# A fused attention and feed-forward kernel on one Trainium2 core: in the first block, big loads wait for TensorE's products, and the block's steps are written in a new order

## The chip, the cores and the metric

The kernel runs on one core of one Trainium2 chip. The metric is the device time of one execution in microseconds (us). TensorE (PE) multiplies matrices, VectorE (DVE), ScalarE (ACT) and GpSimd (POOL) work element by element; SyncE (SP), ACT and POOL also issue DMAs.

## What is computed

`x` is 32 x 64 x 512, float32. Two stages follow one another, each on a layer norm of its input and each added to its input:

```python
x = x + xattn(layernorm(x), ctx, ctx, Wq, bq, Wk, bk, Wv, bv, Wo, bo)
x = x + ffn(layernorm(x), gate, up, down)
# xattn, for every sample: q = Wq x + bq, k = Wk c + bk, v = Wv c + bv   (64 x 64 weights)
#   8 heads over the 512 columns: p = softmax(q_h k_h^T / 8), 64 x 64;  out = Wo (p v_h) + bo
# ffn: each weight is (int32 - int32 zero) * scale, zeros and scales per group of 128 rows
#   out = (silu(h gate) * (h up)) down,   gate, up: 512 x 1792, down: 1792 x 512
```

## The kernel before

Two samples make a pair (128 partitions: 2 x 64 rows), there are 16 pairs, and four pairs make a block of 512 rows (PB = 4), so four blocks. For each block the kernel runs attention, then the feed-forward stage; the attention of block t + 1 is threaded into the feed-forward of block t, which takes 14 slices of 128 columns (gate_up, L588, and down, L629). The first block has no feed-forward to hide in, and its attention is done alone: that is the part that the change touches.

**The first block.** Its steps are methods of class Attention (L322), one object for each of the pairs 0 to 3: stats, scale, apply (layer norm on DVE, the power on POOL, DVE); k, q, v (projections on PE) with k_out, q_out (DVE) and v_out (ACT); scores (PE), highest and less (DVE), exp (ACT), sums (DVE), divide (POOL); turn (PE: weights of the softmax, transposed, times Wo) and turn_out (ACT); weigh (PE), residual (DVE, and a DMA of x1 to DRAM from SP); stats2, scale2, apply2 (second layer norm); flip (PE transposes), high (ACT) and low (DVE), which leave the transposed input of the feed-forward stage in two parts hTh and hTl, so that the float32 product is done as two. PE products take four PSUM tiles of two banks in turn (pool ps0).

**The written order.** The string START (L734) lists these steps with the pair's number, and the loop at L774 issues them one by one under a manual schedule: each engine gets its instructions in this order, and each engine works its own queue in order. Names without a number are common steps: projections, biases and scales prepare constants; zeros (zeros_to_dram, L147) casts the zero points on POOL, writes them to DRAM from SP and, in the kernel before, also issues the broadcast load of the first 512 columns' zeros to all partitions (load_zeros, L272: three DMAs from SP, 512, 512 and 256 KB) and the rows of x of the next two pairs (load_rows, L123: one DMA of 512 KB from SP); weights (load_weights, L265) issues three DMAs of 1 MB each from POOL, one behind the other: the integers of gate, up and down for the first 512 of the 1792 columns; integers is one step of weight_steps (L286): POOL subtracts the zeros from a 128 x 512 piece of gate or up (four such steps stand near the end of START); quotients (L232) prepares scale ratios on DVE.

**After the first block** the order within each engine comes from the framework's planner, which goes by the order of the program text and by its own estimates of times. A few calls pin instructions behind others (issue_after); `newest` keeps, for each engine, the last instruction of the first block's steps or of the main loop, behind which POOL's later loads and subtractions are put. Down's pieces are subtracted on DVE (L301), gate's and up's on POOL (L295), each block of 512 columns after its zeros have been reloaded into the one buffer z.

Of the kernel before, what the change touches and what calls it, by code (L numbers as in the profile page):

```python
# [1 line left out]

# [24 lines left out]
def kernel(  # L27
# [41 lines left out]
    nc = tc.nc  # L69
    B, D, L = x.shape  # L70
    I = gate_w.shape[1]
    P = 128
# [5 lines left out]
    PB = 4  # L78
    NBLK = NPAIR // PB
    TB = PB * P  # L80
    SET = 2
# [32 lines left out]
    with ExitStack() as fast:  # L114
        const = fast.enter_context(tc.tile_pool(name="const", bufs=1))
        rows = fast.enter_context(tc.tile_pool(name="rows", bufs=1))
        att = fast.enter_context(tc.tile_pool(name="att", bufs=1))
        blk = fast.enter_context(tc.tile_pool(name="blk", bufs=2))
        zeros = fast.enter_context(tc.tile_pool(name="zeros", bufs=1))
        xs, hTh, hTl = {}, {}, {}  # L120
        newest = {}

        def load_rows(j: int, pairs: list = [range(SET)]):  # L123

            xs[j] = rows.tile([P, SET, L], F32, tag="x", name=f"x_{j}", bufs=3)
            for some in pairs:
                load_pairs(xs[j], x_rows, j, some)

        def load_pairs(dst: bass.AP, src: bass.AP, j: int, some: range):
            a, b = some.start, some.stop  # L130
            return nc.sync.dma_start(dst[:, a:b, :], src[:, j * SET + a : j * SET + b, :]).ins
# [5 lines left out]
        def places(pool):  # L137
            return {n: pool.tile([P, SET, L], F32, tag=n, name=f"{n}_set") for n in PARTS}
# [27 lines left out]
        wide = [(c, min(CW, I - c)) for c in range(0, I, CW)]  # L166
# [3 lines left out]
        def projection_loads():  # L170
            w_nat = early.tile([D, 5, D], F32, tag="w_nat", name="w_nat")
            b_nat = early.tile([1, 6, D], F32, tag="b_nat", name="b_nat")
            for i, w in enumerate((Wk, Wv, Wq, Wo)):
                nc.scalar.dma_start(w_nat[:, i, :], w)
            for i, b in ((1, bk), (0, bq), (2, bv), (4, bo)):
                nc.gpsimd.dma_start(b_nat[:, i, :], b.unsqueeze(0))
            nc.gpsimd.tensor_copy(w_nat[:, 4, :], w_nat[:, 0, :])
            for i in (2, 4):
                nc.scalar.copy(b_nat[:, i + 1, :], b_nat[:, i, :])
            return w_nat, b_nat  # L180
# [37 lines left out]
        def scale_loads():  # L218
            s_nat = early.tile([NS, 3, P], F32, tag="s_nat", name="s_nat")
            for m, s in enumerate((gate_s, up_s, down_s)):  # L220
                nc.sync.dma_start(s_nat[:, m, :], s.rearrange("g (c p) -> (g c) p", p=P))
            return s_nat
# [33 lines left out]
        ng = const.tile([P, KT, I], F32R, tag="ng", name="ng")  # L256
        nu = const.tile([P, KT, I], F32R, tag="nu", name="nu")
        nd = const.tile([P, FC, L], F32R, tag="nd", name="nd")
        n_sum = []

        gate_rows = gate_w.rearrange("(g p) i -> p g i", p=P)
        up_rows = up_w.rearrange("(g p) i -> p g i", p=P)
        down_rows = down_w.rearrange("(f p) l -> p f l", p=P)

        def load_weights(at: int, n: int):  # L265

            c, fs = slice(at, at + n), slice(at // P, (at + n) // P)
            nc.gpsimd.dma_start(ng[:, :, c], gate_rows[:, :, c])
            nc.gpsimd.dma_start(nu[:, :, c], up_rows[:, :, c])
            newest["POOL"] = nc.gpsimd.dma_start(nd[:, fs, :], down_rows[:, fs, :]).ins  # L270

        def load_zeros(at: int, n: int):  # L272
            z16 = zeros.tile([P, 2, KT, CW], BF16, tag="z16", name=f"z16_{at}")
            z8 = zeros.tile([P, KT, CW], U8, tag="z8", name=f"z8_{at}")
            for m in range(2):
                nc.sync.dma_start(
                    z16[:, m, :, :n], z_rows[m, :, at : at + n].partition_broadcast(P)
                )
            nf = n // P
            zd = z8_dram[at // P * L : (at // P + nf) * L]  # L280
            nc.sync.dma_start(
                z8[:, :nf, :].rearrange("p f l -> p (f l)"), zd.partition_broadcast(P)
            )
            return z16, z8

        def weight_steps(zs):  # L286

            for i, (at, n) in enumerate(wide):
                if i:
                    zs = load_zeros(at, n)  # L290
                z16, z8 = zs
                for g in range(KT):
                    for m, dst in enumerate((ng, nu)):
                        piece = dst[:, g, at : at + n]
                        nc.gpsimd.tensor_tensor(  # L295
                            piece, piece.bitcast(F32), z16[:, m, g, :n], ALU.subtract
                        )
                        yield
                for i in range(n // P):
                    piece = nd[:, at // P + i, :]  # L300
                    nc.vector.tensor_tensor(piece, piece.bitcast(F32), z8[:, i, :], ALU.subtract)  # L301
                    yield
# [424 lines left out]
        def chain(*gens):  # L727
# [4 lines left out]


        START = """  # L734
            0.stats 0.scale 0.apply 1.stats projections 1.scale biases 1.apply
            projections_out 2.stats 0.k biases_out 2.scale 3.stats 0.q 1.k 0.q_out
            3.scale 1.q 0.k_out zeros 2.apply 0.scores 1.q_out 2.k 0.highest 0.less
            2.k_out 0.exp 1.k_out 0.sums 2.q 3.apply 3.k 0.divide 2.q_out 3.q
            3.k_out weights 2.scores 3.q_out 0.turn 2.highest 3.scores 0.turn_out
            2.less 1.scores 3.highest 2.exp 3.v 3.less 1.highest 0.v 3.exp 1.less  # L740
            3.v_out scales 2.sums 1.v 0.v_out 1.exp 3.sums 2.v 2.divide 1.v_out
            0.weigh 1.sums 3.divide scales_out 2.v_out 0.residual 0.stats2 2.turn
            1.divide 3.turn 2.turn_out 2.weigh 3.turn_out quotients 0.scale2 1.turn
            2.residual 2.stats2 3.weigh 1.turn_out 1.weigh 1.residual 1.stats2
            2.scale2 0.apply2 1.scale2 2.apply2 0.flip 3.residual 3.stats2 2.flip
            0.high 2.high 1.apply2 3.scale2 integers integers integers integers
            0.low 1.flip 3.apply2 2.low 1.high 3.flip 1.low 3.high 3.low
        """
        place = places(att)
        with (  # L750
            tc.tile_pool(name="early", bufs=1) as early,
            tc.tile_pool(name="att0", bufs=1) as att0,
            tc.tile_pool(name="ps0", bufs=4, space=bass.MemoryType.PSUM) as ps0,
            tc.manual_schedule(),
        ):
            w_nat, b_nat = projection_loads()
            at_first = [place, places(att0)]
            for j in range(PB // SET):
                load_rows(j, [])
            for p in range(PB):  # L760
                j, i = divmod(p, SET)
                load_pairs(xs[j], x_rows, j, range(i, i + 1))
                load_pairs(at_first[j]["c"], c_rows, j, range(i, i + 1))
            for m, z in enumerate((gate_z, up_z, down_z)):
                nc.sync.dma_start(z_nat[:, m, :], z.rearrange("g (c p) -> (g c) p", p=P))
            s_nat = scale_loads()
            make_block(0)

            def first_banks(name: str):
                return ps0.tile([P, 2, CW], F32, tag="s", name=name)  # L770

            pairs = [Attention(p, 1, at_first[p // SET], first_banks) for p in range(PB)]
            halves = {}
            for step in START.split():  # L774
                if step[0].isdigit():
                    getattr(pairs[int(step[0])], step[2:])()
                elif step == "weights":
                    load_weights(*wide[0])
                elif step == "zeros":
                    zeros_to_dram()  # L780
                    weights = weight_steps(load_zeros(*wide[0]))
                    load_rows(PB // SET)
                elif step == "integers":
                    next(weights)
                elif step == "quotients":
                    quotients()
                elif step.endswith("_out"):
                    next(halves[step[:-4]], None)
                else:
                    halves[step] = {  # L790
                        "projections": lambda: projections(w_nat),
                        "biases": lambda: biases(b_nat),
                        "scales": lambda: scales(s_nat),
                    }[step]()
                    next(halves[step])
# [70 lines left out]
    with tc.If(nc.values_load(flag, min_val=0, max_val=1) != 0), ExitStack() as slow:  # L866
# [20 lines left out]
        for at, n in wide:  # L887
            c = slice(at, at + n)
# [86 lines left out]
```

## Time and profile before

| what | value |
|---|---|
| median of 3 runs | 458.27 us (457.67 to 458.99) |
| profiled execution, own time | 457.47 us |
| its span, first to last instruction | 454.7 us |
| mean granted TensorE clock | 0.97 of full |
| busy: PE, DVE, ACT, POOL | 414.0, 331.5, 309.1, 280.0 us |
| last hTl of the first block, on DVE | starts at 44.11, takes 0.69 us |
| first product of the feed-forward stage, on PE | starts at 44.90 us |
| three weight loads of the first block issued on POOL | at 18.18, 19.03, 19.78 us |
| zeros' broadcast, rows of x issued on SP | at 12.82 to 13.87, at 14.37 us |

The profile is of one execution. Busy time says how long an engine had an instruction in work; a wait is put down to what released it, and "issue" is idle time in which an engine waited for nothing that the profile shows. In the page's slices each digit is a fortieth of the span (11.4 us), in tenths. The page's chain follows the work that ended last back from the end. Where the busy times of stretches are shown, the columns are: the stretch, its length, then busy us (and count of instructions) of PE, of PE's weight loads, of DVE, ACT and POOL, then the granted clock, the mean share of 16 DMA engines and GB/s. DMA queues are q1 (issued from SP), q0 (issued from POOL) and q8 (kind "instruction").

### The profile page before, as it was taken

Reading aid. Unit: us, or ns where it says so; the run is one execution under the profiler, and the core shown is the slowest. Engines: PE = TensorE matmul, PEld = TensorE weight load, DVE = VectorE, ACT = ScalarE, POOL = GpSimd, SP = SyncE. Lnnn points to the kernel's source line nnn. Section 1 sums busy time; section 2 is a strip of 40 time slices with the busy share of each in tenths; the row PEclk is TensorE's granted clock in tenths of the full one; section 3 lists DMA queues with packets and bytes.
Section 4 is the critical chain, followed back from the end, with each engine's and each line's share of the span. In section 5 each row is a group of like instructions: output and inputs, shape, how many; then the busy total and the mean of one; then the engine's idle time right before and its main releaser. Section 6 shows DMA issues by size and latency. Waiting matters only on the chain.

```text
span 454.7 us, 10323 instructions
## 1 busy us (share of the span) xinstructions
PE 414.0 (91%) x4175; PEld 316.3 (70%) x4175; DVE 331.5 (73%) x510; ACT 309.1 (68%) x473; POOL 280.0 (62%) x293
## 2 busy tenths in 40 slices
PE   4755998998999999999999899999999999999991
PEld 4743564766677776777778577786778888887871
DVE  4878653797979983696869775586869655668673
ACT  2142589665787669686788569786688778777760
POOL 5335739658474487676787686764566887783311
PEclk9885899999999999999999999999999999999997
DMA  6793779436102020141000012130001012100004
GB/s 207 234 306 137 217 227 257 130 105 183 54 22 77 1 94 1 46 140 50 1 16 32 2 48 94 48 94 1 1 1 48 1 47 86 54 1 0 1 2 146
DMA packets 20928, 36.55 MB, mean 80 GB/s; under 512 B 1848, under 2 KB 7432, under 8 KB 20872
## 3 DMA queue, kind: packets, MB, share of 16 engines
q1 hardware_dynamic: 14056, 24.20, 16.0%
q0 software_dynamic: 6208, 11.01, 8.6%
q8 instruction: 35, 0.57, 0.5%
q10 hardware_dynamic: 608, 0.59, 0.4%
q14 instruction: 21, 0.17, 0.1%
HBM read 27.37 MB, written 8.42 MB: 79 GB/s over the span
## 4 chain that ended last, share of the span: by engine, by line
PE 43%; POOL 25%; issue 14%; DVE 10%; DMA 3%; ACT 3%; ACTq 0%; POOLq 0%; SPq 0%; DVEq 0%
PE pu L597 10%; PE pg L597 10%; POOL hl L624 7%; PE pd L642 6%; PE pd L645 5%; POOL squares L318 4%; POOL squares L316 4%; POOL hh L623 3%; DVE xn_set L112 3%; DVE y L653 2%; DMA z<-z_dram 2%; POOL q_e_set L481 2%; POOL nu L295 2%; POOL ng L295 1%; DVE k_eT_set L404 1%
## 5 line engine op out<-in xcount | busy, mean ns | idle before, releaser
L653 DVE SCALAR_TENSOR_TENSOR y<-pd,s_all,y 128x512 f32<-128x512 f32 x204 | 150.1, 743 | 47.0 <-PE pd L645 44.2
L607 ACT ACTIVATE pg<-pg,s_q 128x512 f32<-128x512 f32 x168 | 111.5, 665 | 74.2 <-PE pg L597 72.9
L607 ACT ACTIVATE pu<-pu,s_q 128x512 f32<-128x512 f32 x168 | 110.8, 660 | 4.1 <-PE pu L597 4.1
L642 PE MATMUL pd<-hh,nd 128*128 128x512 f32 x224 | 93.9, 419 | 1.6 <-DVE y L653 1.1
L597 PE MATMUL pg<-hTh,ng 128*128 128x512 f32 x224 | 91.2, 407 | 4.5 <-POOL ng L295 1.4
L623 POOL CAST hh<-h 128x512 fp32r<-128x512 f32 x55 | 35.1, 637 | 92.3 <-DVE h L613 90.7
L597 PE MATMUL pu<-hTh,nu 128*128 128x512 f32 x224 | 90.3, 403 | 0.8 <-POOL nu L295 0.5
L597 PE MATMUL pg<-hTl,ng 128*128 128x512 f32 x224 | 89.3, 399 | 0.0
L597 PE MATMUL pu<-hTl,nu 128*128 128x512 f32 x224 | 88.9, 397 | 0.0
L645 PE MATMUL pd<-hl,nd 128*128 128x512 f32 x224 | 88.7, 397 | 0.1
L624 POOL TENSOR_TENSOR hl<-h,hh 128x512 fp32r<-128x512 f32 x55 | 72.0, 1309 | 4.4
L613 DVE SCALAR_TENSOR_TENSOR h<-pu,s_all,g 128x512 f32<-128x512 f32 x56 | 41.8, 747 | 34.3 <-ACT g L610 27.8
L318 POOL TENSOR_TENSOR squares<-squares 128x512 f32<-128x512 f32 (+1 forms) x46 | 55.1, 1197 | 1.7
L597 PEld LDWEIGHTS pg<-hTh,ng 128*128 128x128 f32 x224 | 42.2, 189 | 18.3 <-ACT pg L607 3.9
L642 PEld LDWEIGHTS pd<-hh,nd 128*128 128x128 f32 x224 | 42.0, 188 | 18.0 <-DVE y L653 5.0
L597 PEld LDWEIGHTS pu<-hTh,nu 128*128 128x128 f32 x224 | 42.2, 188 | 13.9 <-ACT pu L607 2.8
L597 PEld LDWEIGHTS pu<-hTl,nu 128*128 128x128 f32 x224 | 42.2, 188 | 9.9 <-issue 0.4
L597 PEld LDWEIGHTS pg<-hTl,ng 128*128 128x128 f32 x224 | 42.4, 189 | 9.0
L610 ACT ACTIVATE g<-pg,s_all 128x512 f32<-128x512 f32 x56 | 38.8, 693 | 13.9 <-PE pg L597 12.1
L645 PEld LDWEIGHTS pd<-hl,nd 128*128 128x128 f32 x224 | 42.1, 188 | 7.9 <-POOL hl L624 0.5
L295 POOL TENSOR_TENSOR ng<-ng,z 128x512 fp32r<-128x512 f32 (+1 forms) x16 | 16.6, 1040 | 8.0 <-DMA z<-z_dram 8.0
L295 POOL TENSOR_TENSOR nu<-nu,z 128x512 fp32r<-128x512 f32 (+1 forms) x16 | 17.1, 1069 | 0.0
(290 smaller groups left out, 484.0 us busy)
## 6 DMA issues: line engine op xcount, KB each, us to landing
z<-z_dram SPq DMA_DIRECT2D x6, 512.0 KB
x<-in_x_dram SPq DMA_DIRECT2D x6, 512.0 KB
ng<-in_L_ffn_gate_w_dram POOLq DMA_DIRECT2D x3, 1024.0 KB, 5.9
nu<-in_L_ffn_up_w_dram POOLq DMA_DIRECT2D x3, 1024.0 KB, 7.7
nd<-in_L_ffn_down_w_dram POOLq DMA_DIRECT2D x3, 1024.0 KB, 10.6
c_set<-in_ctx_dram SPq DMA_DIRECT2D x6, 512.0 KB
x_dram<-x SPq DMA_DIRECT2D x6, 512.0 KB
r<-x_dram SPq DMA_DIRECT2D x6, 512.0 KB
```

The source lines that it names most:

```text
L295: nc.gpsimd.tensor_tensor(piece, piece.bitcast(F32), z16[:, m, g, :n], ALU.subtract)
L316: nc.gpsimd.tensor_tensor(square[:, :n], piece, piece, ALU.mult)
L318: nc.gpsimd.tensor_tensor(total[:, :n], total[:, :n], square[:, :n], ALU.add)
L597: nc.tensor.matmul(acc, w[:, g, ts(f, P)], half[:, g, :], start=(g == 0 and half is hi), stop=(g == KT - 1 and half is lo), skip_group_che ...
L607: nc.scalar.activation(acc, acc, AF.Copy, scale=by)
L610: nc.scalar.activation(g_sb, acc, AF.Silu, scale=by)
L613: ins = nc.vector.scalar_tensor_tensor(h_sb, acc, by, g_sb, ALU.mult, ALU.mult)
L623: nc.gpsimd.tensor_copy(hh, h_sb)
L624: ins = nc.gpsimd.tensor_tensor(hl, h_sb, hh.bitcast(F32), ALU.subtract)
L642: nc.tensor.matmul(pd, w, h_hi[t, f], start=(t, f) != LAST, stop=False, skip_group_check=True)
L645: nc.tensor.matmul(pd, w, h_lo[t, f], start=False, stop=True, skip_group_check=True)
L653: ins = nc.vector.scalar_tensor_tensor(y, pd, by, y, ALU.mult, ALU.add)
```

## The change

The load of the three weights is cut into single steps, gate, up and down; so is what zeros issued: broadcast (the three zeros' DMAs) and rows. Four of them, broadcast, up, rows and down, stand in a context behind_products: the first instruction that they issue gets a true dependency (a semaphore wait) on the last PE instruction traced before it. So in the new order the broadcast waits for 1.scores, up for 3.k, rows for 0.turn and down for 3.turn. Gate has no such wait. On its queue the whole load stands behind its first DMA. START is written anew: pairs 0 and 1 come ahead of pairs 2 and 3 in most steps (before, pair 1's scores and turn came after those of pairs 2 and 3), gate stands where zeros stood and zeros follows it, down is issued late in the block, and the four integers stand ahead of 2.apply2, 3.apply2 and quotients. No operation on data is added or removed.

```diff
+        def load_wide(w: bass.AP, src: bass.AP, at: int, n: int):
+            newest["POOL"] = nc.gpsimd.dma_start(w[:, :, at : at + n], src[:, :, at : at + n]).ins
+
+        def load_down(at: int, n: int):
+            fs = slice(at // P, (at + n) // P)
+            newest["POOL"] = nc.gpsimd.dma_start(nd[:, fs, :], down_rows[:, fs, :]).ins
+
         def load_weights(at: int, n: int):
-            c, fs = slice(at, at + n), slice(at // P, (at + n) // P)
-            nc.gpsimd.dma_start(ng[:, :, c], gate_rows[:, :, c])
-            nc.gpsimd.dma_start(nu[:, :, c], up_rows[:, :, c])
-            newest["POOL"] = nc.gpsimd.dma_start(nd[:, fs, :], down_rows[:, fs, :]).ins
+            load_wide(ng, gate_rows, at, n)
+            load_wide(nu, up_rows, at, n)
+            load_down(at, n)
...
         START = """
-            0.stats 0.scale 0.apply 1.stats projections 1.scale biases 1.apply
-            projections_out 2.stats 0.k biases_out 2.scale 3.stats 0.q 1.k 0.q_out
-            3.scale 1.q 0.k_out zeros 2.apply 0.scores 1.q_out 2.k 0.highest 0.less
-            2.k_out 0.exp 1.k_out 0.sums 2.q 3.apply 3.k 0.divide 2.q_out 3.q
-            3.k_out weights 2.scores 3.q_out 0.turn 2.highest 3.scores 0.turn_out
-            2.less 1.scores 3.highest 2.exp 3.v 3.less 1.highest 0.v 3.exp 1.less
-            3.v_out scales 2.sums 1.v 0.v_out 1.exp 3.sums 2.v 2.divide 1.v_out
-            0.weigh 1.sums 3.divide scales_out 2.v_out 0.residual 0.stats2 2.turn
-            1.divide 3.turn 2.turn_out 2.weigh 3.turn_out quotients 0.scale2 1.turn
-            2.residual 2.stats2 3.weigh 1.turn_out 1.weigh 1.residual 1.stats2
-            2.scale2 0.apply2 1.scale2 2.apply2 0.flip 3.residual 3.stats2 2.flip
-            0.high 2.high 1.apply2 3.scale2 integers integers integers integers
-            0.low 1.flip 3.apply2 2.low 1.high 3.flip 1.low 3.high 3.low
+            0.stats 0.scale 0.apply 1.stats projections 1.scale biases
+            projections_out 1.apply 2.stats 0.k biases_out 2.scale 3.stats 0.q 1.q
+            0.k_out 3.scale 0.q_out 1.k gate zeros 1.q_out 0.scores 1.k_out 2.k
+            3.apply 1.scores broadcast 0.highest 2.apply 2.k_out 0.less 0.v
+            1.highest 0.exp 2.q 1.less 0.v_out 3.q 0.sums 1.exp 2.v 2.q_out 0.divide
+            3.k up 2.v_out 1.sums 2.scores 3.q_out 1.divide 3.k_out 1.v 2.highest
+            3.scores 1.v_out 2.less 1.turn 3.highest 2.exp 0.turn rows 3.less
+            1.turn_out 2.sums 3.exp 1.weigh 0.turn_out 3.sums 2.divide 3.v
+            1.residual 1.stats2 3.divide 0.weigh 3.v_out 2.turn 0.residual 0.stats2
+            1.scale2 3.turn down 2.turn_out 2.weigh 3.turn_out 1.apply2 0.scale2
+            scales 2.residual 2.stats2 3.weigh scales_out 1.flip 3.residual 3.stats2
+            2.scale2 1.high 0.apply2 3.scale2 integers integers integers integers
+            2.apply2 0.flip 1.low 2.flip 3.apply2 0.high quotients 3.flip 2.high
+            0.low 3.high 2.low 3.low
         """
...
+            @contextmanager
+            def behind_products():
+                traced = nc.cur_bb.bb.instructions
+                last = next(i for i in reversed(traced) if i.engine == mybir.EngineType.PE)
+                n = len(traced)
+                yield
+                first = traced[n]
+                tc.add_manual_dep(
+                    first,
+                    last.name,
+                    mybir.DependencyInfo(
+                        mybir.DependencyClass.Sync, mybir.DependencyReason.DATA
+                    ),
+                    reason="behind products",
+                )
...
-                elif step == "weights":
-                    load_weights(*wide[0])
+                elif step == "gate":
+                    load_wide(ng, gate_rows, *wide[0])
                 elif step == "zeros":
                     zeros_to_dram()
-                    weights = weight_steps(load_zeros(*wide[0]))
-                    load_rows(PB // SET)
+                elif step == "broadcast":
+                    with behind_products():
+                        weights = weight_steps(load_zeros(*wide[0]))
+                elif step == "up":
+                    with behind_products():
+                        load_wide(nu, up_rows, *wide[0])
+                elif step == "rows":
+                    with behind_products():
+                        load_rows(PB // SET)
+                elif step == "down":
+                    with behind_products():
+                        load_down(*wide[0])
```

More of the change, by code (lines that the diff above doesn't have):

```diff
@@ L1 @@
-from contextlib import ExitStack
+from contextlib import ExitStack, contextmanager
 import concourse.bass as bass
```

## The prediction

> **What bounds the kernel now.** I read the page's forty slices first, then the chain of work that ended last over the first 46 us, then who waited for whom on VectorE (DVE) there, then busy time by stretch, then the DMA queues of short stretches. Overall TensorE (PE) is busy for 91% of the span, but the change touches only the first 45 us, and there the slices show something else:
>
> ```profile
> PE   4755998998999999999999899999999999999991
> DVE  4878653797979983696869775586869655668673
> PEclk9885899999999999999999999999999999999997
> ```
>
> Slices are 11.4 us wide. In the second PE has 7 tenths and DVE 8; in the third and fourth PE falls to 5, and its granted clock falls with it. The chain says what happens inside:
>
> ```profile
> 28.15 0.47 PE po L506 x32
> 28.62 0.28 PE pe L490 x10
> 28.90 3.48 issue
> 32.38 0.81 PE pe L490 x13
> ```
>
> PE stops after 10 of the 32 products of 1.turn, waits for no semaphore, and goes on 3.48 us later. DVE runs dry behind it (columns: total, times, longest, over 0 to 44.85 us):
>
> ```profile
> DVE st L368 <- DMA x<-in_x_dram: 3.6, 1, 3.6
> DVE x L518 <- PE po L506: 3.4, 1, 3.4
> DVE xn_set L112 <- POOL rs L374: 1.4, 2, 0.8
> DVE mx L455 <- PE pss L444: 1.4, 2, 1.1
> DVE hTl L543 <- ACT hTh L539: 0.6, 1, 0.6
> DVE q_e_set L404 <- PE pq L393: 0.4, 1, 0.4
> ```
>
> These six are all of DVE's idle time in the block: 10.8 us. Everything else is work, so **DVE's queue sets the block's end** (last hTl at 44.11 + 0.69 = 44.80 us; the first gate product starts at 44.90), plus what it waits for.
>
> Why does PE stop? Cutting the stretch where PE has gaps with no releaser (19.99, 26.05, 32.38) gives the matmuls between them:
>
> ```profile
> 0.00:19.95 19.95, 11.42 (x346) 10.51 (x346) 13.76 (x30) 3.04 (x6) 8.96 (x23) 0.95 0.65 207
> 19.95:26.03 6.08, 4.62 (x127) 3.53 (x127) 4.82 (x10) 4.02 (x8) 1.24 (x2) 0.87 1.19 358
> 26.03:32.30 6.27, 2.54 (x126) 2.27 (x127) 5.40 (x15) 1.93 (x4) 3.35 (x5) 0.96 1.09 341
> ```
>
> First two pairs: PE and its weight loads. The gaps stand 127+127 and 126+127 instructions apart: [...]so they are borders of instruction blocks, reached after matmuls 346, 473 and 599. The queue of kind "instruction" (q8) carries such blocks: between 24 and 30 us it has no packet, in 30 to 32 us it has one, while the third big load (down) drains:
>
> ```profile
> q1 hardware_dynamic: 298, 0.56, 74.5%
> q8 instruction: 1, 0.02, 3.0%
> q0 software_dynamic: 11, 0.01, 2.3%
> ```
>
> Before that, q0 alone (three 1 MB weight loads issued back to back at 18.18, 19.03 and 19.78) took 132 and 134% of the engines in 24:26 and 26:28. So the fetch of the block after 599, due when PE passed 473 at 26.05, came after the weights, and too late.
>
> [...] The 3.48 us stop is followed by a clock of 0.50 from 32 to 48 us. [...] Here an apply takes 0.54 us, and 1.29 us at 40.99, beside POOL's integers.
>
> **The change part by part.** I call T0 the end of the last hTl, 44.80 now, and count how it moves.
>
> *The waits on loads.* Counting matmuls in the new order (10 up front; 32 for each k, q, scores, turn, weigh; 8 for a v): 3.k ends at 346, 0.turn covers 451 to 482, 3.turn 587 to 618, 1.scores 203 to 234. If the borders stay at 346, 473 and 599, and one stride earlier at 219, each of the four waiting loads (zeros broadcast behind 1.scores, up behind 3.k, rows behind 0.turn, down behind 3.turn) is issued just after PE has entered a new block, so the fetch is asked for ahead of the load. The block after 599 is then due about 4.3 us after 473: DVE's 3.highest 0.69, 3.less 0.69, 2.sums and 3.sums 0.86 each, then about 1.0 for 3.divide (POOL, 3.04 for three) and part of the turn; now it is 2.8 us. In front of that fetch lie up's rest, rows and context, 0.5 MB each, not 3 MB. I take the stop as gone: **-3.44** on DVE. If part of it stays, cover is under rival B.
>
> *What queues behind the waiting instructions.* On POOL, up holds 1.divide; 3.k follows 2.v with no late input, and 0.divide occupies POOL meanwhile: 0, plus the 0.75 us of the issue itself, which 3.scores covers (1.turn comes after it). Down holds 0.scale2, which nobody needs before 0.apply2, four DVE steps later: 0. Gate's issue (0.85) moves ahead of the casts of the zeros (0.39 and 0.29) and so of their way through DRAM; integers need them some 20 us later: 0. On SP the broadcast (three DMAs) and rows (one) hold the next context load and the writes of x1; the first reader of these is the next block: 0. Without these covers each would cost its own length, 0.7 to 0.9 us.
>
> *The written order.* Pair 1 is now finished early, and between a PE step and its reader on DVE there are one to three other DVE steps. Waits that may go: 0.63 (last hTl; now two lows and quotients stand before) and 1.4 + 0.4 (highest, q_out). The first I count whole, the other two half, since new short waits can appear: **-0.63 - 0.9**; bounds -0.6 and -2.4. The 1.4 of the first applies stays: that part of the order is the same.
>
> *Contention it adds.* integers now stand before 2.apply2, 3.apply2 and quotients; now only one apply runs beside them. One more apply at 1.29 - 0.54 = **+0.75**; quotients (0.23 + 0.68 + 0.24) may double: 0 to 1.15, [...]**+0.3**.
>
> *Clock.* Between the last weigh and T0 PE has only flips in both orders, so the entry is at half clock either way. Now it lasts 4.0 us past T0 (the 2 us from 48 on have a mean clock of 0.79, so full speed returns at about 48.8); [...]the chain there runs through DVE, POOL and DMA, not PE. **+0.2**[...].
>
> Sum: -3.44 - 0.63 - 0.9 + 0.75 + 0.3 + 0.2 = **-3.7 us**. After T0 nothing in the chain is tied to the clock of the start: rs_4to, the next weight issues, integers, the reload of zeros (8.19 us) all hang on T0, so the shift reaches the end. The profiled execution took 457.47 us (span 454.7, 2.8 around it) and would take 453.8; it is 0.8 below the median of 458.27, for which the same step gives **454.5 us**.
>
> **Rivals.** A, the above: 452.0 to 456.2 (the waits all gone, no quotient cost, -5.5, and a little from what is planned after; or only the stop and the 0.63 gone, with half of the unknown costs: -3.44 - 0.63 + 0.75 + 0.55 + 0.7 = -2.1, 456.2). Chance 0.70.
>
> B, the fetch is still late, somewhere in 3.turn, by the whole 3.5 us. DVE then still has 1.stats2's rest, 0.residual 0.87, 0.stats2 1.1 and 1.apply2 0.54, about 2.5 us, before it needs 2.weigh; PE needs 1.0 for the rest of 3.turn and 2.weigh. Cover 1.5, exposed 2.0: 454.5 + 2.0 = 456.5, range 455.5 to 457.3. For it: context and rows are still on the queues then. Against: the borders found above. Chance 0.14.
>
> C, the change doesn't do what it is meant to, or the gain is spent right after T0: the zeros' reload (8.19 us beside 3 MB of weights) ends where it did. Then 458.3, within 457.2 to 459.5. Against: the reload starts on POOL's last nu, which follows T0. Chance 0.10.
>
> D, slower: down is issued last, some 10 us later than now (19.78, against about 28.5, taken from 3.turn's end, 28.15 now). Its reader is DVE's nd subtraction (45.99 now, 1.1 after the first gate product; then about 42.3), and behind it on DVE stands rs_4to, on which POOL's next loads wait. Now down's load of this block lands 11.3 us after issue, behind gate and up; alone it should need less. 28.5 + 0.75 + 11.3 = 40.6, still in time. Each us past 42.3 costs one; it is slower than before from a landing at about 46: at 48, 460.2. Chance 0.06.
>
> **How the numbers follow.** The forecast is A's. Range 452.0 to 457.2: A and B to their ends; C and D, 0.16, are left out. About 0.3% (1.4 us) is what a measurement of this kernel can tell from no change. Faster: A and six sevenths of B, 0.82; same: the rest of B and C, 0.12; slower: D, 0.06.
>
> **What would show it.** Right: no issue gap over 1 us on PE before T0; q8 packets soon after matmuls 346 and 473; DVE's idle time under 7 us, the po wait gone; two applies near 1.3 us; the first gate product near 41 us. Wrong: T0 moves by 4 and the end does not (C); a PE gap inside 2.turn or 3.turn (B); DVE idle at nd for a DMA (D).

## The result, and the profile after

| kernel | median, us (runs, lowest to highest) | ratio to before, 95% interval |
|---|---|---|
| before, same chip | 459.12 (20, 457.62 to 462.02) | |
| after | 457.19 (20, 454.44 to 458.89) | 0.995, 0.9931 to 0.9969 |

The change is worth some 2 us, where 3.7 were forecast. The profiled execution of after took 457.63 us (span 455.3), beside 457.47 (span 454.7) in the one of before that is shown: these two executions do not show the gain at all. The first gate product of the feed-forward stage (a matmul into pg) starts at 43.85, not at 44.90 and not "near 41". The ninth, which opens the second slice of 128 columns, starts at 56.66, against 56.52, and up to the last gate product the distance between the two executions stays at 0.1 us. The spans are 0.6 apart, but they are a poor measure here: the own time less the span is 2.73 us in the mean of the 130 runs of before whose span is on record, and 2.29 in the 44 of after. Own times and starts of products are compared below.

The page's slices of after, the rows PE, DVE and PEclk:

```profile
PE   4854998998999999999999899999999999999991
DVE  5959553797979983696869775586869655668672
PEclk9988799999999999999999999999999999999996
```

The third slice (from 22.8 us) still has PE at 5 tenths, and now DVE is at 5 tenths with it. The chain of waits shows that PE still stops, in another place:

```profile
22.10 0.57 PE pe L497 x23
22.67 5.15 issue
27.82 0.50 PE pe L497 x9
28.32 0.90 PE po L513 x32
29.24 0.89 DVE x L525 x2
```

PE stops after 23 of the 32 products of 0.turn. 0.turn covers matmuls 451 to 482, so this is after 473: the border before the one that stopped it in before. At 599 PE does not stop any more, as was predicted. Who waited for whom on DVE, up to 45 us (total, times, longest):

```profile
DVE x L525 <- PE po L513: 4.3, 1, 4.3
DVE st L375 <- DMA x<-in_x_dram: 3.8, 2, 3.6
DVE xn_set L112 <- POOL rs L381: 1.4, 2, 0.8
DVE k_eT_set L411 <- PE pk L400: 0.2, 1, 0.2
```

The short waits for highest, q_out and the last hTl are gone; the long one has grown from 3.4 to 4.3. The busy times by stretch, cut at border 346, at the stop, at the first and the ninth gate product (columns as under "Time and profile before"):

```profile
0.00:18.70 18.70, 11.15 (x346) 9.78 (x346) 12.99 (x29) 4.92 (x9) 7.35 (x21) 1.00 0.62 186
18.70:22.67 3.97, 3.18 (x127) 2.38 (x128) 3.87 (x8) 1.38 (x4) 2.40 (x3) 1.00 0.91 293
27.82:43.85 16.03, 9.21 (x229) 7.66 (x228) 14.13 (x32) 4.99 (x9) 8.09 (x9) 0.80 0.77 234
43.85:56.66 12.81, 11.71 (x160) 7.27 (x161) 7.45 (x15) 6.21 (x9) 8.28 (x9) 0.73 0.79 220
```

Again 346 and then 127 matmuls, so the borders are where the prediction had them. That a block is fetched one block ahead was read by the prediction from before, and this trace agrees: the next two packets of the queue of kind "instruction" (q8) come at 28.9 and 32.4, 1.1 and 1.0 us after PE has passed 473 (27.82) and 599 (31.40). By this the block after 473 is asked for when PE passes 346, at 18.7. The queues' rows of four stretches, 17 to 18.7, 18.7 to 23, 23 to 25.3 and 25.3 to 27.9 us:

```profile
q1 hardware_dynamic: 18, 0.02, 3.1%
...
q1 hardware_dynamic: 1131, 1.22, 93.4%
...
q0 software_dynamic: 315, 0.65, 88.5%
q1 hardware_dynamic: 51, 0.07, 22.0%
...
q1 hardware_dynamic: 243, 0.48, 53.4%
q0 software_dynamic: 210, 0.40, 47.3%
q8 instruction: 1, 0.02, 2.3%
```

Just ahead of the border the engines are idle. Then the zeros' broadcast (1.22 MB on q1) fills them, then up (q0), and the q8 packet comes 6.6 us after the border, at 25.3 (it ends at 26.25; PE goes on at 27.82). Why these two loads lie there is seen in the issues on SP and POOL (start, length, engine and line, what):

```profile
11.08 0.81 POOL L267 DMA_DIRECT2D ng<-in_L_ffn_gate_w_dram  x1
...
12.33 0.33 SPq L150 DMA_DIRECT2D z_dram<-z  x1
12.76 0.34 SPq L151 DMA_DIRECT2D z_dram<-z  x1
17.24 0.95 SPq L283 DMA_DIRECT2D z<-z_dram  x2
18.29 0.45 SPq L288 DMA_DIRECT2D z<-z_dram  x1
...
19.23 0.82 POOL L267 DMA_DIRECT2D nu<-in_L_ffn_up_w_dram  x1
```

The products of 1.scores, for which the broadcast waits by the change, were through at 14.60. It is issued at 17.24, because it also reads what the zeros wrote to DRAM, and that small write stood behind gate's 1 MB. SP's own waits name it (total, times, longest):

```profile
SPq L283 <- DMA z_dram<-z: 4.1, 1, 4.1
```

And 3.k ends exactly at matmul 346, so the wait of up holds it only to the end of the old block (18.42). POOL was still at a divide, and issued up 0.5 us after PE had passed the border.

### The profile page after: what moved, and what is told of

It is laid out like the page before. It is cut to its first block, busy times and chain, and to the rows that moved or that the text cites. A ratio compares the mean times of both kernels' runs of the same rounds, so it can differ in the third digit from the quotient of the medians.

```text
span 455.3 us, 10322 instructions
## 1 busy us (share of the span) xinstructions
PE 413.0 (91%) x4175; PEld 315.3 (69%) x4175; DVE 330.5 (73%) x510; ACT 309.3 (68%) x473; POOL 280.4 (62%) x293
## 4 chain that ended last, share of the span: by engine, by line
PE 45%; POOL 23%; issue 15%; DVE 10%; ACT 4%; DMA 1%; ACTq 0%; POOLq 0%; DVEq 0%
PE pg L604 11%; PE pu L604 11%; PE pd L649 6%; POOL hl L631 6%; PE pd L652 5%; POOL squares L325 4%; POOL squares L323 4%; POOL hh L630 3%; DVE xn_set L112 2%; DVE y L660 2%; POOL nu L302 2%; POOL q_e_set L488 1%; POOL ng L302 1%; DVE k_eT_set L411 1%; DMA w_nat<-in_L_xattn_Wo_dram 1%
```

## The experiments

In the expectations, theory F is the mechanism of the prediction: the fetch of a block of instructions waits for data that are queued, and PE stops when the block is not there. The other letters are rivals.

**Both kernels profiled again.** Nothing is edited; the question is what varies. The columns: own time of the profiled execution, PE's stops of over 1 us at a border (from the start of the last matmul to that of the next, and after which matmul), start of the first and of the ninth gate product.

| execution | own time | stops | first | ninth |
|---|---|---|---|---|
| before, shown | 457.47 | 3.70 (599) | 44.90 | 56.52 |
| before_again | 458.40 | 3.05 (599) | 43.92 | 57.31 |
| before_third | 457.54 | 2.78 (599) | 42.95 | 56.29 |
| before_fourth | 458.20 | 4.38 (346), 1.37 (473), 1.44 (599) | 45.40 | 57.08 |
| before_fifth | 459.55 | 3.56 (346), 1.98 (599) | 45.61 | 59.00 |
| before_sixth | 457.50 | 3.89 (599) | 44.42 | 55.90 |
| after, shown | 457.63 | 5.36 (473) | 43.85 | 56.66 |
| after_again | 458.05 | 5.90 (473) | 44.65 | 57.35 |
| after_third | 458.41 | 5.09 (473) | 44.37 | 57.10 |
| after_fourth | 455.81 | 5.09 (473) | 43.45 | 54.87 |

> The kernel before once more, for its profile alone: its timed runs go from 456.1 to 462.4 us, and the profile shown is from the fast end (457.47). Theory F: the place of the stop depends on which transfers a block's fetch meets, so another execution shows a stop of another length, 3 to 6 us, after matmul 473 or 599. Theory C [...]: the same stop of 3.5 us after 599, first gate product at 44.9, and a half clock that lasts 4 to 8 us past it.

> The same, once more, with the same expectations: F, a stop of 3 to 6 us in another place or of another length; C, the same stop and only another clock.

> The kernel before, for a profile of one of its longer executions (its runs go up to 462 us, the three profiles so far took 457.5 to 458.4). Theory F: if it takes over 459.5, a stop of 5 us or more, or two stops, between matmuls 346 and 599. Theory C: the stop is 3 us and the clock after it is low for longer.

> The same once more: F, over 459.5 us only with a stop of 5 us or more or two stops; C, with the stop of 3 us and a longer low clock.

> The kernel before once more. Theory F: stops of 3 to 7 us in all, after 346 or 599, first gate product 43 to 46. If its long executions (460 to 462 us) are those with stops at more than one border, one that takes 460 us or more shows over 6 us of stops and a first gate product after 46.

> The changed kernel once more, for how far one profile of it stands for others. Theory F (the fetch of the instruction block after matmul 473 waits behind the zeros' broadcast and the up load, which are issued at 17.2 to 20.1 us, over the border at matmul 346): the same order of transfers, so a PE stop of 4 to 6 us again after matmul 473 and a first gate product at 43 to 45 us. Theory R (the stop is an accident of one execution): another place or no stop. Time 0.992 to 0.998 of the kernel before under both.

> The changed kernel once more, a look at its spread. Theory F: one stop of 5 to 6 us after matmul 473, the first gate product at 43.5 to 45. Rival V (the place of the stop varies as it does in the kernel before, and the medians' 2.3 us come from executions without it): no stop over 3 us, first gate product below 42.

> As after_third: by theory F a stop of 5 to 6 us after matmul 473 and the first gate product at 43.5 to 45; by rival V no such stop and below 42.

In before the place of the stop is a matter of the execution: four times at 599, twice at 346. The chain of before_fourth, where it fell in 0.turn's first half:

```profile
18.55 0.23 PE pe L490 x16
18.78 4.16 issue
22.94 0.71 PE pe L490 x16
```

In after it is at 473 in all four profiles, and 5.1 to 5.9 us long; rival V of after_third (executions without the stop) found no support. Timed again in 22 runs, after had a median of 457.51 us and a ratio of 0.9951 (0.9931 to 0.997). before_sixth did not catch a long execution: before took 460 us or more in 55 of its 150 timed runs, after in 0 of 44, but none of the six traces of before is of such a run. The longest of them, before_fifth with 459.55, has stops over 1.9 us at two borders, which is what theory F had asked of an execution over 459.5.

One thing narrows down where executions differ: in all 20 traces of this document, of every kernel, the own time less the start of the ninth gate product is 400.3 to 401.6 us, and the last gate product starts 380.4 to 380.8 us after the ninth. What made these executions long or short lies ahead of the ninth product.

**Gate and zeros exchanged (zeros_first).** The small write goes ahead of gate's 1 MB.

```diff
-            0.k_out 3.scale 0.q_out 1.k gate zeros 1.q_out 0.scores 1.k_out 2.k
+            0.k_out 3.scale 0.q_out 1.k zeros gate 1.q_out 0.scores 1.k_out 2.k
```

> The changed kernel with zeros ahead of gate, so that the small write of the zeros to DRAM is not behind gate's 1 MB. Theory F: the broadcast goes out at about 14.7 us, right behind 1.scores, drains by about 20, and the fetch asked for at matmul 346 (18.3 us) comes before 22.5: the stop after 473 shrinks from 5.15 us to under 1.5 us, and the first gate product moves from 43.85 to about 41; time 0.988 to 0.993 of before. Rival P (PE's blocks can't come faster than one in so many us, whatever else is on the queues): the stop stays at 4 to 5 us. Rival M (the broadcast now meets gate, and the fetch at matmul 219 is late instead): a stop of 2 us or more after 346, and a gate product at 42 to 44.

Measured: 457.06 us (12 runs), ratio 0.9935 (0.9905 to 0.9965). The broadcast is issued at 14.83, 2.4 us earlier, but now gate is ahead of its data, which drain from 16.7 to 21; up follows. The packet comes at 24.33, and PE's stop after 473 is 4.27 us, of which DVE waits 3.2. This edit takes away a fifth of the stop: border 346 is still under load. Theory F had forecast less than 1.5 us; the number is the one of rival P, which only later runs (mended, weights_late) rule out.

**Up behind rows (up_later).** Only the step up is moved, from 3.k to behind 0.turn and rows.

```diff
-            3.scores 1.v_out 2.less 1.turn 3.highest 2.exp 0.turn rows 3.less
+            3.scores 1.v_out 2.less 1.turn 3.highest 2.exp 0.turn rows up 3.less
```

> The changed kernel with up issued behind 0.turn (matmul 473), together with rows, and no more behind 3.k. Theory F: the fetch asked for at 346 waits for the broadcast alone and comes at about 23.3 in place of 25.3 to 26.2; the stop after 473 falls from 5.4 to 5.9 us to 2 to 3.5, the first gate product to about 41.5 to 42.5. Theory Z (the broadcast alone holds the fetch, up is behind it anyway): the stop stays at 5 us or more. Time 0.990 to 0.995.

455.42 us (7), 0.9901 (0.9866 to 0.9937). The broadcast, issued at 18.12, still straddles border 346; without up behind it the packet comes at 23.92, and the stop is 3.17 us (DVE: 2.1). The stop and the first gate product (42.32) are as theory F had them. Up costs the fetch 2 us here: its packet comes 4.6 us after border 346, in after 6.6.

**Both (mended), and the weights split otherwise (gate_mid).** mended: zeros ahead of gate, and up behind 2.scores instead of 3.k, one step past the border (that line is shown). gate_mid: zeros early, gate behind 2.scores and with a wait for it, up and down behind 3.turn.

```diff
...
-            3.k up 2.v_out 1.sums 2.scores 3.q_out 1.divide 3.k_out 1.v 2.highest
+            3.k 2.v_out 1.sums 2.scores up 3.q_out 1.divide 3.k_out 1.v 2.highest
```

> The changed kernel with two edits: zeros ahead of gate (as in zeros_first) and up behind 2.scores in place of 3.k, which ends just at the border after matmul 346, so that up could start before PE asked for the next block. Theory F: at that fetch (asked for at about 18.7) only the rest of the broadcast is ahead, it comes at 20 to 22 us, the stop after 473 is under 1.5 us (4.27 in zeros_first, 3.17 with up later alone), first gate product at 40 to 41.5; time 0.986 to 0.991. Theory B (any load between 346 and 473 delays it, ahead or not): the stop stays at 3 us or more, 0.990 to 0.995.

> Zeros alone early, gate behind 2.scores (with a wait), up and down behind 3.turn. Weights_late had no stop, and lost 2.5 us where DVE waited for down. Theory F: gate drains between the borders 346 and 473, no stop over 1 us, up and down land by about 36, DVE's wait for down goes; first gate product at about 38.5, entry to the next stage 2 us earlier than in weights_late; 450 to 452 us against 453, 0.980 to 0.985 of before. Theory E (the wait for down was covered anyway): the same time as weights_late, 0.987.

454.34 us (6), 0.9895 (0.9854 to 0.9936), and 454.13 us (6), 0.9892 (0.9854 to 0.993). The stop after 473 is gone in both; a stop of 1.7 us at 599 is left, and DVE waits only 0.2 for it. The first gate product is at 40.43 and 39.82. mended came in as theory F had it; gate_mid did not (450 to 452 us and no stop over 1 us were expected).

**All weights late (weights_late).** Zeros early; gate, up and down all behind 3.turn, where a long list of DVE work is still to come.

```diff
...
-            1.scale2 3.turn down 2.turn_out 2.weigh 3.turn_out 1.apply2 0.scale2
+            1.scale2 3.turn gate up down 2.turn_out 2.weigh 3.turn_out 1.apply2 0.scale2
```

> The changed kernel with gate, up and down all behind 3.turn (the border after matmul 599), so that until then only the zeros' broadcast, the next context and rows use the queues, and the zeros' small write is behind nothing. Theory F: broadcast out at about 14.7, drained by 19.5; the fetch asked for at 346 comes at about 20, no stop over 1 us after 473 or 599, DVE waits under 7 us in all, first gate product at 39.5 to 41 (or when the integers are done, if up lands late: to 42). Time 0.987 to 0.992 of before. Rival P (PE's blocks have a pace of their own): a stop of 3 us or more stays.

453.01 us (6, 452.91 to 454.76), 0.9868 (0.9832 to 0.9904): the lowest median, though its interval overlaps those of mended, gate_mid and weights_mid. No stop over 1 us at any border, against rival P; the packets come at 19.32, 23.82 and 27.73, 0.7 to 1.5 us after the borders; the first gate product at 38.55. DVE's three longest waits, up to 46 us:

```profile
DVE st L375 <- DMA x<-in_x_dram: 3.8, 2, 3.6
DVE nd L308 <- DMA nd<-in_L_ffn_down_w_dram: 2.5, 1, 2.5
DVE xn_set L112 <- POOL rs L381: 1.4, 2, 0.8
```

With the stop gone the next thing is late: down's data, rival D's mechanism, here a wait of 2.5 us inside a gain.

**Down a little earlier (weights_mid).** Gate behind 0.turn (with a wait for it), up and down behind 1.scale2, ahead of 3.turn.

```diff
...
-            1.scale2 3.turn down 2.turn_out 2.weigh 3.turn_out 1.apply2 0.scale2
+            1.scale2 up down 3.turn 2.turn_out 2.weigh 3.turn_out 1.apply2 0.scale2
```

> The new order with zeros early; gate behind 0.turn, just behind matmul 473, up and down behind 1.scale2, ahead of 3.turn. Theory F: no stop over 1 us, since every load is issued behind a border and has a block's time to drain; gate, up and down land 1 to 4 us earlier than in weights_late, so DVE's wait for down (2.5 us) and POOL's for up (2.9) fall below 1 and the time is 451 to 453 us. Rival (the late landing in weights_late was hidden, or 3 MB of loads take as long wherever they start): 453 to 454.5 as weights_late and gate_mid.

453.05 us (6), 0.9878 (0.9838 to 0.9918): no better. Up and down were issued no earlier than in weights_late, so the earlier landing that had been expected did not come. Down was issued at 28.96, as in weights_late (28.88). Gate's wait for 0.turn held POOL for 3.9 us (a stop of 1.48 us at 473 lay in it), and with it the divides and the later issues, 2.divide among them (25.60, against 24.15). Then down landed 14.4 us after its issue:

```profile
28.17 0.74 POOL nu L267
28.91 0.06 issue
28.96 14.44 DMA nd<-in_L_ffn_down_w_dram
43.41 0.02 issue
43.43 0.69 DVE nd L308
```

**The order alone, the loads alone.** new_order_old_loads has the new order with zeros, broadcast and rows together and the three weights together behind 3.k, without waits for products. old_order_paced has the old order with gate where zeros stood, and the paced loads at the like borders.

```diff
-            0.k_out 3.scale 0.q_out 1.k gate zeros 1.q_out 0.scores 1.k_out 2.k
-            3.apply 1.scores broadcast 0.highest 2.apply 2.k_out 0.less 0.v
+            0.k_out 3.scale 0.q_out 1.k zeros broadcast rows 1.q_out 0.scores 1.k_out 2.k
+            3.apply 1.scores 0.highest 2.apply 2.k_out 0.less 0.v
...
-            3.k up 2.v_out 1.sums 2.scores 3.q_out 1.divide 3.k_out 1.v 2.highest
+            3.k gate up down 2.v_out 1.sums 2.scores 3.q_out 1.divide 3.k_out 1.v 2.highest
...
```

> The steps in the new order, the loads as before: zeros, broadcast and rows together and without a wait, gate, up and down back to back behind 3.k in the written order, without a wait. Theory F: 3 MB of weights are queued at 19 to 21 us as before, the fetch for the border at 599 comes at about 30 and PE stops for 3 to 4 us in 3.turn, of which 1.5 to 2.5 us reach DVE; first gate product at 42.5 to 44; time 0.992 to 0.999. Rival O (the order brings the whole gain of the change): 0.993 to 0.997, like the changed kernel.

> The steps in the order of the kernel before, the loads paced as in the changed one: gate ahead of zeros, the others each behind the product in which one of the borders (matmuls 219, 346, 473, 599) lies in that order: 2.q, 0.turn, 0.weigh, 1.turn. Theory F: the three weights no longer stand back to back before the fetch for 599, so the stop of 3.48 us there goes or falls under 1.5 us; but broadcast and up follow one another over 346 as in the changed kernel, so a stop of 2 to 5 us after 473. Time 0.993 to 1.000. Rival O (the new order, not the pacing, brings the gain): no gain, 0.998 to 1.003, with a stop at 599 as before.

457.74 us (22, 453.59 to 459.65), 0.9947 (0.9921 to 0.9972), and 456.9 us (10), 0.994 (0.9907 to 0.9973). As far as these intervals tell, each half gives what the whole gives; they do not add. Rival O of the first (the order brings a gain like the whole one) is borne out by the time. The trace of new_order_old_loads is of one of its short executions (454.2 us), 3.5 us under its median:

```profile
26.99 0.46 PE pe L497 x14
27.45 2.29 issue
29.73 0.50 PE pe L497 x17
```

A stop at 599 of 2.3 us (theory F had 3 to 4), and DVE waits only 0.8 for it (3.4 of 3.5 in before): in the new order DVE has some 1.5 us of other work there. old_order_paced has one stop, 2.74 us after 346 (DVE waits 2.6); its packet came at 18.73. Theory F had put that stop after 473; rival O, with a stop at 599 and no gain, failed too.

**The old order without loads in the way (old_order_late, old_order_clear).** Zeros early, rows behind 0.weigh, all weights behind 1.turn. The broadcast stands behind 2.q in the first and behind 3.scores in the second; the lines show this one step, from the first (-) to the second (+).

```diff
-            2.k_out 0.exp 1.k_out 0.sums 2.q broadcast 3.apply 3.k 0.divide 2.q_out 3.q
-            3.k_out 2.scores 3.q_out 0.turn 2.highest 3.scores 0.turn_out
+            2.k_out 0.exp 1.k_out 0.sums 2.q 3.apply 3.k 0.divide 2.q_out 3.q
+            3.k_out 2.scores 3.q_out 0.turn 2.highest 3.scores broadcast 0.turn_out
```

> The written order of before, with the zeros and their broadcast early (broadcast behind 2.q), rows behind 0.weigh and all three weights behind 1.turn, the last PE step of the first block that is long. Theory F (a fetch waits behind the data already queued): no stop of PE over 1 us after matmuls 346, 473 and 599, first gate product 39.5 to 41, time 454 to 456 us; what is then left between it and weights_late (453.0 us, 38.55) is the order's own share, 1 to 2 us, from the short waits of DVE that only the old order has (0.63 + 1.4 + 0.4). Rival O (the order is worth nothing by itself): the time is 453 to 453.7. Rival P (the stop does not come from the queued loads): a stop of 2.5 us or more stays, and 457 to 458.

> old_order_late with one step moved: the zeros' broadcast (1.25 MB) stands behind 3.scores, well behind matmul 346, in place of 2.q, which starts right at matmul 219. Theory F (the stop after matmul 346 in old_order_late was the fetch asked for at 219, behind that broadcast): fetch packet for the block after 346 by 16 us, no stop over 1 us at any border, median 453.5 to 455 and a range of runs below 4 us. What is left to weights_late (453.0) is then the order's own share, 0.5 to 2 us. Rival O (the old order carries a stop of its own): a stop of 2.5 us or more stays and the median is 456 to 457.5.

old_order_late: 456.8 us (22, 453.12 to 459.62), 0.9934 (0.9908 to 0.996). The stop that theory F had as gone was there, after 346 (the trace is of a long execution, 459.17 us):

```profile
18.63 0.23 PE pe L497 x16
18.86 3.07 issue
21.93 0.71 PE pe L497 x16
```

The broadcast was issued 0.5 us after border 219, and the packet came 5.7 us after that border, behind it. In weights_late the same 0.5 us had been enough (packet after 1.0 us). Moving the broadcast alone, in old_order_clear, brings the packets of the first two borders to 14.55 and 19.62, 0.1 and 0.5 us after them, and the stop at 346 is gone: so it did not belong to the old order. But the forecast of the time failed: 456.74 us (22), 0.9967 (0.9946 to 0.9988). The broadcast now drains over border 473 (packet 2.5 us after it, stop of 1.68 us at 599), and down, issued last at 31.09, is what DVE waits for:

```profile
DVE nd L308 <- DMA nd<-in_L_ffn_down_w_dram: 4.0, 1, 4.0
...
DVE mx L462 <- PE pss L451: 0.6, 2, 0.3
DVE hTl L550 <- ACT hTh L546: 0.5, 2, 0.3
DVE q_e_set L411 <- PE pq L400: 0.5, 1, 0.5
```

The last three, 1.6 us, are short waits that weights_late, in the new order, does not have.

## Why the prediction was wrong

The step that failed is "I take the stop as gone: -3.44". PE stopped for 5.2 us after matmul 473 in place of 3.5 after 599, and DVE's wait for PE rose from 3.4 to 4.3 us. The account of DVE up to the first gate product, and of what follows (us; the third column compares the two executions shown, the fourth the means of the six profiles of before and the four of after):

| term | taken | shown pair | means |
|---|---|---|---|
| DVE's wait for PE's stops | -3.44 | +0.9 | +0.6 (3.8 to 4.35) |
| short waits | -1.53 | -2.2 | -1.3 |
| applies beside integers | +0.75 | -0.45 | |
| quotients beside integers | +0.3 | +1.1 | |
| first to ninth gate product | +0.2 | +1.2 | -0.1 (12.5 to 12.4) |

The first four rows sum to -0.65 for the pair shown, where the first gate product moved by -1.06; the rest has no single term.

1. **The waiting loads.** "each of the four waiting loads ... is issued just after PE has entered a new block, so the fetch is asked for ahead of the load" holds for rows and down (28.38 and 32.20; PE passed the borders at 27.82 and 31.40). The broadcast got its product in time, but not its data: it was issued 3.1 us after border 219 and drained over 346. Up's product, 3.k, ends exactly at 346, so its wait puts nothing of the new block ahead of it; it was issued 0.5 us after the border. That was too little with the broadcast there (zeros_first, packet 5.6 us after the border); 1.0 us, one step later, was enough (mended, 1.6).
2. **Gate's place in the queue.** "Gate's issue (0.85) moves ahead of the casts of the zeros and so of their way through DRAM; integers need them some 20 us later: 0." The wrong reader was asked. The write's next reader is the broadcast, issued at 12.82 in before and, after a wait of 4.1 us for that write, at 17.24 in after; so it moved over border 346, and the one who paid was the instruction fetch. zeros_first, up_later and mended take the two causes away one by one and together: the stop at 473 is 5.1 to 5.9 us in after, then 4.3, 3.2 and 0.4; the time 457.2 to 457.5, then 457.1, 455.4 and 454.3.
3. **The mechanism** was right: a fetch that comes behind queued loads stops PE. With the loads taken from border 346 the stop at 473 goes (from 5.1 to 5.9 us in after to under 1 in weights_late, mended and gate_mid), and moving one broadcast moves the stop from one border to another (old_order_late, old_order_clear). Rival B ("the fetch is still late, somewhere in 3.turn", 456.5, to 457.3) is the nearest: its cover of 1.5 is what the new order has at 599 (mended, gate_mid: stop of 1.7, DVE's wait 0.2). But the stop fell in 0.turn, where DVE had only 1.0 us of cover (5.36 against 4.3), and was longer.
4. **The written order.** -1.53 was right in kind and size: -2.2 against the shown execution, -1.3 in the means.
5. **Contention.** Its sum, +1.05, came out at +0.65, with the parts exchanged. "quotients may double" came true (1.15 to 2.24), and the value of +0.3, near 0, was wrong. The second apply beside the integers, priced at +0.75, did not come: one runs beside them in after too, and takes 0.84 in place of 1.29. The lines of after, beside POOL's integers from 38.28 on:

```profile
38.88 0.84 DVE L112 TENSOR_SCALAR xn_set<-x,mv,rs 128x512 f32<-128x512 f32 x1
39.64 1.19 DVE L236 SCALAR_TENSOR_TENSOR s_inv<-s_all 128x84 f32<-128x84 f32 x1
40.87 0.68 DVE L237 RECIPROCAL s_inv<-s_inv 128x84 f32<-128x84 f32 x1
41.58 0.37 DVE L238 TENSOR_TENSOR s_q<-s_all,s_inv 128x84 f32<-128x84 f32 x1
```

Two of the three quotients went from 0.23 and 0.24 to 1.19 and 0.37; the reciprocal, 0.68, did not change. The price beside the integers differs by operation, and what sets it no trace shows.

6. **The clock.** That "the entry is at half clock either way" did not hold in the shown execution of after (granted clock 1.00 from 41.11 to 44.52, 0.50 from there to 51.35). The half clock ended 4.0 us past the first gate product in before and 7.5 in after; the price of +0.2, like the +0.7 in rival A's sum, was an estimate of the author, and the shown pair has +1.2. But in the six profiles of before the half clock ended 3.6 to 8.1 us past, so the shown one was a short case and this is no effect of the change. That "the chain there runs through DVE, POOL and DMA, not PE" is doubtful for this stretch: in the ten profiles of the two kernels the ninth product came 11.4 to 11.7 us after the first where the half clock ended 3.4 to 4.1 us past it (four), and 12.7 to 13.4 where it ended 6.5 to 8.1 past it (six). No run sets the clock, so which of the two brings the other is not shown.
7. **Where the measured 2 us are.** In the means of the profiles, first gate product, ninth and own time of after are 0.5, 0.5 and 0.6 us earlier; in the timed runs it is 2. The profiled executions are not typical: those of before have a mean of 458.1 us, its 150 timed runs one of 459.3 (the sum was made on an execution of 457.47); those of after have 457.5, its 44 runs 457.2. All of the runs are lower, not only the long ones: the quartiles are 457.84, 459.25 and 460.64 in before, 456.38, 457.28 and 458.07 in after. If own times differ by what lies ahead of the ninth product in the untraced executions too, the rest of the gain lies there, in stops or in the clock. That the executions of 460 us and more are those with stops at two or three borders fits before_fifth and is not shown, since no trace caught one. It stays open, as does what the order is worth where no stop is left: weights_late and old_order_clear differ by 1.9 us at the first gate product (38.55, 40.45), and by more in time, but down is later in the second, and it still has a stop.

## What to carry to other kernels

An instruction fetch is one more transfer (in after one packet of 0.02 MB on q8), and in this kernel it was due one block (about 127 matmuls with their weight loads) after it was asked for; its packet came 0.1 to 1.1 us after the border on nearly idle queues, and 3.0 to 7.2 us after it where the other queues moved 1.2 MB or more. So mark the borders of the blocks in the written order, and let no large load be issued, or still be draining, there. A wait that is to put a load behind a border must be for a product well past it (0.5 us was enough in weights_late, not in old_order_late; 1.0 us was in mended and gate_mid), and the load's other inputs must be ready by then; a small write on which a broadcast depends is put ahead of a large load, not behind (the broadcast waited 4.1 us for it in after, 0.6 in mended). When a stop is predicted as gone, look at each border for itself, since the stop can move to another one over which loads drain.

## What the runs showed that was not expected

- How late a fetch gets: over the 20 traces and borders 219, 346 and 473, the fetch's packet came 0.1 to 1.1 us after the border in the 13 cases in which the other queues moved less than 0.1 MB until then, and 3.0 to 7.2 us after it in the 19 in which they moved 1.2 MB or more (the rest lie between, but for one packet at its border, old_order_paced at 473). The bytes grow with the wait, so this gives no rate; it shows that no fetch was late on idle queues. No run shows what holds it.
- A load issued 0.5 us after a border can be ahead of the fetch or behind it (old_order_late 5.7 us, weights_late 1.0).
- A block's packet took 0.9 to 1.6 us, and where PE stood waiting it went on 1.3 to 1.6 us after the packet's end (26.25 to 27.82 in after, 20.54 to 21.93 in old_order_late).
- In before the same program stopped at different borders from one execution to the next, so one profile was a poor sample: its first gate product varied from 42.95 to 45.61 us.
